# Every engine's queue in text order: a two-layer convolution kernel without its instruction planner

## The chip, the cores and the metric

The kernel runs on one core of a Trainium2 chip. The metric is the device time of one execution in microseconds, here 9654.11 us, the median of 3 runs (9645.51 to 9654.31). The engines are called as in the profile: PE (TensorE, matrix products), DVE (VectorE), ACT (ScalarE), POOL (GpSimd) and SP (SyncE, which only issues transfers). Each takes its instructions from a queue in a fixed order, and an instruction that waits holds up those behind it.

## The reference

Input x is 32 images of 96 channels, 56 x 56 points, fp32. Two layers follow each other.

```
# layer 0: expand, depthwise 3x3, squeeze-and-excite, project, residual (weights rounded to 8 bits)
h = silu(bn(conv1x1(x, q(w1))))                     # 96 -> 576 channels
h = silu(bn(depthwise3x3(h, q(w2))))
s = sigmoid(se_w2 @ silu(se_w1 @ mean(h) + b1) + b2)
x = x + bn(conv1x1(h * s, q(w3)))                   # 576 -> 96

# layer 1: attention from spectra, deformable 3x3 convolution, batch norm over all images
mag = abs(rfft2(x));  fe = mean over channels of mag, resized
ca  = sigmoid(mlp(pooled, separably filtered mag))               # one per channel
sa  = sigmoid(small convs of [mean(x), sqrt(mean(x*x)), fe])     # one per point
y   = x * ca * sa
freq_e = mean over channels of abs(rfft2(y)), resized
aux = [y, 4 coordinate planes, freq_e]
offset = conv3x3(aux);  gate = sigmoid(conv1x1(relu(conv3x3(aux))))
z = (1 - gate) * conv3x3(y) + gate * deformable_conv3x3(y, offset)   # bilinear samples
out = relu(batchnorm(z) + x)
```

## The kernel before

**Image pipeline.** Image b goes through three streams at once. *First* (`hidden`, L203) expands image b+2 with matmuls (`expand`, L168, silu on ACT L172) and runs the depthwise convolution on DVE: nine taps (L259, L261) for each of nine units of 128 channels, written to DRAM after a silu (`finish`, L221). *Second* (`attend`, L437) takes image b+1: squeeze (L284 to L296), projection in four steps of two row blocks (`project`, L323 and L329, with loads hq by SP and residuals on POOL), then the spectrum (`dft_mag`, L338: L386 and L410 on PE, squares on ACT L413, sums on DVE L372 and L414, roots L417), the chain of small steps that makes ca and sa (L477 to L557), a second spectrum with the gate (L366 on POOL), and freq_e (L564 to L578). The main loop (L1105) makes z of image b.

**Bands.** The main loop goes over bands of 8 rows, 7 an image. In each band `offsets` (L641) finds the offsets of the band two further on: convolution L605 (offsets, gate's hidden layer, a third of the base convolution), ACT L625 and L628, copies L651 on DVE, base convolution L633, and by way of DRAM the bilinear weights: `ht` (L667 on SP, L670 and L671 on ACT), `hd`, then `weights_load` (L685, L686 on SP) and their product L692 on DVE. A band has two halves. In each, `block_channels` (L696) cuts blocks of y on POOL (L703) and transposes them on PE (L707, out by ACT L709), `sample_tiles` samples by matmul (L721, out by ACT L725) in two groups of three and four tiles, `pack` (L732) moves a third of the taps, and `deform` (L740) makes the product, one half later. `combine` (L779 to L782) ends a band on DVE. The rows of y for the next image are loaded and weighted by `refill` (L584, L592, freq_e L596).

**Slots.** After each tile of a sampling group, and three times at the end of a band, `pump` (L1012) makes a slot: 17 in a band. In a slot each stream takes as many steps as its share of the image's slots asks for; a step ends at a `yield`. At the sixth band of an image (`turn`) the streams move on by one image.

**What sets the order.** The text gives SP's order alone (L1351). For PE, DVE, ACT and POOL a planner of the framework orders the instructions when the kernel is built, by its own costs and by when inputs come free; one place is held to the text by name (L670). After the build each engine's order is fixed. PSUM has 8 banks: 6 that go round (`mm`), one (`acc`) for the small products of `attend`, one (`pd`) for L740.

```
    with tc.manual_schedule(engines={mybir.EngineType.SP}):
        layers(tc, a, dp, x1d, zd, stats, far)
```

Before the first band, image 0 goes through both streams with image 1's first stream beside it, 0.45 steps to one (`beside`, SPREAD). After the last band `normalise` reads all z again and writes the output.

Of the kernel before, what the change touches and what calls it, by code (L numbers as in the profile page):

```python
# [73 lines left out]
UNITS = [(c, 0) for c in range(4)] + [(4, None)] + [(c, 1) for c in range(4)]  # L74

# [127 lines left out]
def hidden(tc, p, x, xn, h2d, pooled, defer):  # L203
# [12 lines left out]
    for _ in expand(nc, p, xts, UNITS[0]):  # L216
        yield
# [8 lines left out]
    for u, (ch, half) in enumerate(UNITS):  # L226
        h1 = p["h1"]
        more = expand(nc, p, xts, UNITS[u + 1]) if u + 1 < len(UNITS) else iter(())
        if xn is not None and u in (5, 8):

            p.setdefault("xts", []).append(rows_of(xn, int(u == 8)))
        acc = p["acch"].tile([128, HH, W], FP, name="acch")
# [5 lines left out]
        if diag is not None:  # L238
# [9 lines left out]
            next(more, None)  # L248
            yield
        for n, k in enumerate(taps):  # L250
# [11 lines left out]
            if n % 2:  # L262
                if n == 3 and before:
                    finish(u - 1, before)
                next(more, None)
                yield
# [12 lines left out]
def squeeze(nc, p, pooled):  # L279
# [3 lines left out]
    for u, (ch, _) in enumerate(UNITS):  # L283
        nc.tensor.matmul(p1[:RED, 0:1], w["sew1"][:, ch], pooled[:, u : u + 1],  # L284
                         start=(u == 0), stop=(u == len(UNITS) - 1))
    s1 = p["sp"].tile([RED, 1], FP, name="s1")
    nc.scalar.activation(s1, p1[:RED, 0:1], AF.Silu, bias=w["seb1"], scale=1.0 / HW)
    yield
    for ch in range(NCH):
        nc.tensor.matmul(p1[:, 8 + ch : 9 + ch], w["sew2"][:, ch], s1, start=True, stop=True)  # L290
    s2 = p["sp"].tile([128, NCH], FP, name="s2")
    nc.vector.tensor_tensor(s2, p1[:, 8 : 8 + NCH], w["seb2"], ALU.add)
    nc.scalar.activation(s2, s2, AF.Tanh, scale=0.5)
    nc.vector.tensor_scalar(s2, s2, 0.5, 0.5, ALU.mult, ALU.add)
# [20 lines left out]
def project(nc, p, rows):  # L315
# [11 lines left out]
    for half in range(2):  # L327
        ps = slice(64 * half, 64 * half + 64)
        nc.tensor.matmul(pts[half][:C, :EW], w3s[ps, NCH - 1], both[ps], start=False, stop=True)  # L329
    outs = []  # L330
# [7 lines left out]
def dft_mag(nc, p, src, gate=None):  # L338

# [3 lines left out]
    if gate is None:  # L351
        parts = p["sq"].tile([2 * WX, 2, NPB * V], FP, name="sq")[: 2 * H, :, : NG * W].rearrange("p k (g w) -> p k g w", g=NG)
# [11 lines left out]
    def weigh(g):  # L364
        if gate is not None and g < NG:
            nc.gpsimd.tensor_tensor(x2s[g][:, :, :W], x2s[g][:, :, :W], gate.unsqueeze(1).to_broadcast([2 * H, CG, W]), ALU.mult)  # L366
# [9 lines left out]
    for _ in range(2):  # L376
        yield
# [3 lines left out]
    if gate is not None:  # L381
        yield
# [13 lines left out]
    if gate is None:  # L396
        p["sums"] = p["sp"].tile([2 * H, 2, W], FP, name="sums")
        nc.vector.tensor_reduce(p["sums"], parts.rearrange("p k g w -> p k w g"), AX.X, ALU.add)
    mag = s1[:, :, :V]
    n = NQB * V  # L400
    pairs = mag.rearrange("p (r q) u -> p r q u", r=2)
    for q0 in range(0, NP // 2, NQB):
# [9 lines left out]
        for r, pt in enumerate(pts):  # L412
            nc.scalar.activation(sq[:, r].rearrange("p k n -> p (k n)"), pt[:, : 2 * n], AF.Square)  # L413
        nc.vector.tensor_tensor(pairs[:, :, q0 : q0 + NQB], sq[:, :, 0].rearrange("p r (q u) -> p r q u", q=NQB),  # L414
                                sq[:, :, 1].rearrange("p r (q u) -> p r q u", q=NQB), ALU.add)
        yield
    nc.scalar.activation(mag, mag, AF.Sqrt)  # L417
    p["magnitude"] = mag


def resized_spectrum(nc, p, mag, name, scale=None):


    m2 = p["sp"].tile([2 * WX, V], FP, name=f"m_{name}")
    if scale is not None:
        nc.vector.tensor_tensor(mag, mag, scale.unsqueeze(2).to_broadcast([2 * WX, NP, V]), ALU.mult)
    nc.vector.tensor_reduce(m2, mag.rearrange("p q u -> p u q"), AX.X, ALU.add)
    yield
    pf = p["acc"].tile([128, 512], FP, name="acc")
    nc.tensor.matmul(pf[:V, : 2 * W], m2, p["w"]["RT2"], start=True, stop=True)  # L430
    rs = p["sp"].tile([V, 2, W], FP, name=name)
    nc.scalar.copy(rs.rearrange("p m w -> p (m w)"), pf[:V, : 2 * W])
    p["resized"] = rs
    yield


def attend(tc, p, b, x, h2d, pooled, x1, given=False):  # L437
# [7 lines left out]
    if not given:  # L445
        NQ = HH // ER
        first = project_loads(nc, p, h2d, 0, 0)
        yield from squeeze(nc, p, pooled)
        rows = [first, project_loads(nc, p, h2d, 0, 1)]
        for _ in range(2):  # L450
            yield
        for q in range(NQ):
# [5 lines left out]
            if q + 1 < NQ:  # L458
                first = project_loads(nc, p, h2d, q + 1, 0)
            yield  # L460
# [7 lines left out]
            yield  # L468
    yield
# [4 lines left out]

    s3 = p["sp"].tile([H, 2, W], FP, name="s3")
    pm = p["acc"].tile([128, 512], FP, name="acc")
    nc.tensor.matmul(pm[:H, : 2 * W], w["fold"], p["sums"].rearrange("p k w -> p (k w)"), start=True, stop=True)  # L477
    nc.scalar.activation(s3[:, 1], pm[:H, W : 2 * W], AF.Sqrt, bias=w["eps6"][:H], scale=1.0 / C)
    nc.scalar.mul(s3[:, 0], pm[:H, :W], 1.0 / C)
    yield  # L480
    yield from resized_spectrum(nc, p, mag, "fe")
    fe = p["resized"]
# [4 lines left out]
    nc.vector.tensor_reduce(edge[:, :, 5:], mag, AX.X, ALU.add)  # L487
    for m in range(2):
# [3 lines left out]


# [5 lines left out]
    pc = p["acc"].tile([128, 512], FP, name="acc")  # L499
    for k in range(3):  # L500
        nc.tensor.matmul(pc[:NP, 8 + 2 * k : 10 + 2 * k], qs[:, 0, k], w["two"], start=True, stop=True)
    g = p["sp"].tile([NP, 3, 2], FP, name="g")
    nc.scalar.copy(g.rearrange("p k c -> p (k c)"), pc[:NP, 8:14])
    yield
    for n in range(6):
        k, c = divmod(n, 2)
        nc.tensor.matmul(pc[: 2 * MID, 0:1], w["cp1"][:, k, c], g[:, k, c : c + 1], start=(n == 0), stop=(n == 5))
    c1 = p["sp"].tile([2 * MID, 1], FP, name="c1")
    nc.scalar.activation(c1, pc[: 2 * MID, 0:1], AF.Relu, bias=w["cp1b"])
    yield  # L510

    nc.tensor.matmul(pc[:C, 1:2], w["cp2"], c1[:MID], start=True, stop=True)
    c2 = p["sp"].tile([2 * MID, 2 * WX], FP, name="c2")
    nc.vector.tensor_scalar(c2, w["twoT"], c1, None, ALU.mult)
    ca = p["ca"].tile([C, 1], FP, name="ca")
    sigmoid(nc, ca, pc[:C, 1:2], w["half"]("cp2_b", C))
    p["ca", b] = ca
    yield
    nc.tensor.matmul(pc[: 2 * WX, 64 : 64 + NP], c2, w["cp2X"], start=True, stop=True)
    cx = p["sp"].tile([2 * WX, NP], FP, name="cx")  # L520
    nc.vector.tensor_tensor(cx, pc[: 2 * WX, 64 : 64 + NP], w["cp2bX"], ALU.add)
    nc.scalar.activation(cx, cx, AF.Tanh, scale=0.5)
    nc.vector.tensor_scalar(cx, cx, 0.5, 0.5, ALU.mult, ALU.add)


    p1 = p["acc"].tile([128, 512], FP, name="acc")
    t1 = p["sp"].tile([W, 3, H], FP, name="t1")
    for m in range(3):
        t = p1[:W, m * H : (m + 1) * H]
# [5 lines left out]
        nc.scalar.activation(t1[:, m], t, AF.Identity, bias=w["sdh_b"](m, W))  # L535
    yield
    p2 = p["acc"].tile([128, 512], FP, name="acc")
    s4 = p["s4"][b % 2]
    for m in range(3):
        nc.tensor.matmul(p2[:H, m * W : (m + 1) * W], t1[:, m], w["twT"][:, m], start=True, stop=True)  # L540
        nc.scalar.activation(s4[:, m, 1 : 1 + W], p2[:H, m * W : (m + 1) * W], AF.Identity, bias=w["sdw_b"](m, H))
    yield
    p3 = p["acc"].tile([128, 512], FP, name="acc")
    r = p["sp"].tile([H, 3, W], FP, name="r")
    for m in range(3):
        for dx in range(3):
# [92 lines left out]


def offsets(nc, p, yp, j, top, hid, ybs, hds):  # L641

    w = p["w"]
# [854 lines left out]
```

## Time and profile before

| | |
|---|---|
| median of 3 runs | 9654.11 us |
| profiled execution, its own time | 9648.5 us |
| its span, first to last instruction | 9646.7 us |
| PE busy | 8472.7 us (88%) |
| PE weight loads | 5064.2 us (52%) |
| DVE busy | 7227.2 us (75%) |
| ACT busy | 5322.1 us (55%) |
| POOL busy | 2532.6 us (26%) |
| PE clock granted, mean | 0.923 |
| DMA | 154 GB/s mean |
| last statistics of image 0, of image 31 | 798.2 us, 9360.7 us |

The profile is of one execution. Busy shares count matmuls, vector and scalar instructions; idle time before an instruction is put down to what released it. A row of a timeline is a run of like instructions. The normalisation fills the time after 9360.7 us.

### The profile page before, as it was taken

The numbers are of one execution on the slowest core, as the hardware profiler recorded it, in microseconds if no ns is written. First come the engines' busy times: TensorE is split into PE (matmuls) and PEld (weight loads), VectorE is DVE, ScalarE is ACT, GpSimd is POOL, SyncE is SP. The second block draws the span as 40 slices with busy tenths as digits, with TensorE's granted clock in tenths as the row PEclk, the third lists the DMA queues.
The fourth block names the chain that finished last, engine by engine and source line by source line (L and its number), as shares of the span: only waits on it lengthen the run. The fifth ranks groups of instructions, "written<-read, shape, count | busy, mean of one in ns | idle before, by whom it ended". The sixth has DMA issues, their size and how long they took to land. (4 is left out here: it accounts for less than half of the span.)

```text
span 9646.7 us, 129705 instructions
## 1 busy us (share of the span) xinstructions
PE 8472.7 (88%) x48374; PEld 5064.2 (52%) x48374; DVE 7227.2 (75%) x6948; ACT 5322.1 (55%) x10262; POOL 2532.6 (26%) x2642
## 2 busy tenths in 40 slices
PE   6889989998999999999899989999999999999870
PEld 3455555555555555555555555555555555555540
DVE  7688777778777787877777887777878777777323
ACT  2355555565555556555555655555555555565453
POOL 1123223222222322222232322233222323322210
PEclk9899999999999999999999999999999999999985
DMA  2355555555555555555555555555555555554449
GB/s 94 95 143 148 151 152 160 150 149 143 147 155 154 160 154 145 145 149 155 154 160 155 145 142 153 151 158 154 153 139 145 150 157 157 153 152 135 130 154 417
DMA packets 1069473, 1485.98 MB, mean 154 GB/s; under 512 B 590438, under 2 KB 840086, under 8 KB 1056550
## 3 DMA queue, kind: packets, MB, share of 16 engines
q1 hardware_dynamic: 858747, 985.20, 37.9%
q10 hardware_dynamic: 153803, 329.80, 9.2%
q0 software_dynamic: 56288, 162.60, 6.7%
q8 instruction: 388, 6.36, 0.3%
q14 instruction: 247, 2.02, 0.1%
HBM read 1064.29 MB, written 412.65 MB: 153 GB/s over the span
## 5 line engine op out<-in xcount | busy, mean ns | idle before, releaser
L261 DVE SCALAR_TENSOR_TENSOR acch<-hp,w,acch 128x1512 f32<-128x1512 f32 (+1 forms) x2250 | 4320.5, 1920 | 32.8
L605 PE MATMUL mm<-yp,c_jointW 104*128 104x448 f32 x4032 | 1649.0, 561 | 9.0 <-ACT yt L709 5.5
L740 PE MATMUL pd<-v,c_def 128*96 128x224 f32 (+1 forms) x6272 | 1414.8, 376 | 127.6 <-ACT v L732 104.1
L703 POOL COPY ybl<-yp 96x448 f32<-96x448 f32 x896 | 1014.7, 1159 | 1903.7 <-PE mm L707 1903.3
L721 PE MATMUL mm<-wc,yt 64*96 64x144 f32 x12544 | 1168.1, 308 | 153.5 <-DVE yb L638 76.8
L740 PEld LDWEIGHTS pd<-v,c_def 128*96 128x96 f32 (+1 forms) x6272 | 1051.8, 173 | 437.4 <-ACT v L732 142.5
L168 PE MATMUL mm<-xt,w 96*128 96x392 f32 (+3 forms) x2688 | 1136.3, 561 | 133.8 <-ACT yt L709 96.0
L605 PEld LDWEIGHTS mm<-yp,c_jointW 104*128 104x128 f32 x4032 | 783.6, 196 | 806.0 <-issue 762.6
L721 PEld LDWEIGHTS mm<-wc,yt 64*96 64x96 f32 x12544 | 884.2, 167 | 489.8 <-issue 188.0
L221 ACT ACTIVATE acch<-acch,sh,inv 128x1568 f32<-128x1568 f32 x288 | 487.5, 1693 | 1159.0 <-DVE acch L261 1143.9
L692 DVE TENSOR_TENSOR wc<-wc,wr 128x1008 f32<-128x1008 f32 x448 | 564.6, 1260 | 704.2 <-DMA wr<-hd 690.5
L725 ACT COPY v<-mm 96x288 f32<-96x288 f32 (+1 forms) x2688 | 1003.6, 442 | 117.7 <-PE mm L721 78.9
L172 ACT ACTIVATE hp<-mm,sh,inv 128x392 f32<-128x392 f32 (+2 forms) x1216 | 811.8, 672 | 326.9 <-PE mm L168 282.1
L633 PE MATMUL mm<-yp,c_base0W 96*64 96x448 f32 x4032 | 913.5, 550 | 0.0
L323 PE MATMUL mm<-hq,w3s 128*96 128x392 f32 x2048 | 788.2, 531 | 127.4 <-DMA hq<-h2d 125.9
L655 POOL DMA_DIRECT2D od<-at x224 | 186.3, 832 | 2275.1 <-DVE at L651 1451.9
L732 ACT COPY v<-v 32x448 f32<-32x448 f32 x1344 | 755.3, 562 | 30.3
L168 PEld LDWEIGHTS mm<-xt,w 96*128 96x128 f32 (+1 forms) x2688 | 389.9, 189 | 495.1 <-issue 264.8
L709 ACT COPY yt<-mm 128x384 f32<-128x384 f32 (+1 forms) x896 | 350.9, 441 | 491.5 <-PE mm L707 489.4
L323 PEld LDWEIGHTS mm<-hq,w3s 128*96 128x96 f32 x2048 | 336.3, 173 | 477.7 <-issue 382.5
L466 POOL TENSOR_TENSOR o<-o,xc 96x392 f32<-96x392 f32 x256 | 396.5, 1549 | 643.9 <-ACT o L333 642.3
L633 PEld LDWEIGHTS mm<-yp,c_base0W 96*64 96x64 f32 x4032 | 294.6, 134 | 515.5 <-issue 490.2
(194 smaller groups left out, 9023.7 us busy)
## 6 DMA issues: line engine op xcount, KB each, us to landing
h2d<-acch ACTq DMA_DIRECT2D x288, 784.0 KB
wc<-hd SPq DMA_DIRECT2D x896, 252.0 KB
wr<-hd SPq DMA_DIRECT2D x896, 252.0 KB
hq<-h2d SPq DMA_DIRECT2D x128, 980.0 KB
hq<-h2d SPq DMA_DIRECT2D x128, 784.0 KB
x<-x1d SPq DMA_DIRECT2D x768, 98.0 KB
ht<-od SPq DMA_DIRECT2D x224, 252.0 KB
hd<-ht ACTq DMA_DIRECT2D x224, 252.0 KB
```

The costliest lines, as they stand in the source:

```text
L168: nc.tensor.matmul(pt[p0 : p0 + w1.shape[1], : rows * W], w1, xts[hf][:, r0 * W : (r0 + rows) * W], start=True, stop=True)
L172: nc.scalar.activation(h1[lo:hi, row0 : row0 + rows, 1 : 1 + W], pt[lo:hi, : rows * W].rearrange("p (h w) -> p h w", h=rows), AF.Silu, bia ...
L261: nc.vector.scalar_tensor_tensor(acc[:, lo:hi], win, wk, acc[:, lo:hi], ALU.mult, ALU.add)
L323: nc.tensor.matmul(pts[half][:C, :EW], w3s[:, ch], hq, start=(i == 0), stop=False)
L605: nc.tensor.matmul(view, weights[:, k], yp[:channels, r0 : r0 + RB, dx + PD - 1 : dx + PD - 1 + W], start=(k == 0), stop=(k == NTAP - 1))
L633: nc.tensor.matmul(pb[k % 2 * BC : (k % 2 + 1) * BC, :BW].rearrange("p (h w) -> p h w", h=RB), w["base"][:, k], yp[:C, r0 : r0 + RB, dx + ...
L692: nc.vector.tensor_tensor(wc, wc, wr, ALU.mult)
L703: nc.gpsimd.tensor_copy(yb[:, :, s], blocks)
L721: nc.tensor.matmul(pt[k][:C, (t - lo) * KP : (t - lo + 1) * KP], yt[ps, t], s[ps, t * KP : (t + 1) * KP], start=True, stop=True)
L725: nc.scalar.copy(v[:C, :, lo:hi, k].rearrange("c k t p -> c t k p"), pt[k][:C, : (hi - lo) * KP].rearrange("c (t k p) -> c t k p", t=hi - ...
L732: nc.scalar.copy(v[C:, 1 + 2 * i : 3 + 2 * i], v[i * QC : (i + 1) * QC, KA:])
L740: nc.tensor.matmul(out.rearrange("c q (t x) -> c t q x", x=TS), p["w"]["def"][ks, k], v[ks, k].rearrange("c t s (r x) -> c t (s r) x", r=T ...
```

## The change

All four compute engines get text order too, and the text is rewritten:

- `pump`: *second* takes exactly one step a slot, *first* one tap's share of 81 steps; a step in `hidden` is now one tap, and the next unit is expanded during the last six taps, the next image's first unit during the last unit.
- In `attend`, `dft_mag`, `squeeze` and `project` an evacuation or a use stands one step after the product that it needs; the products of a chain share one `acc` bank in disjoint columns; the two halves of the chain (ca and sa) are interleaved; the loads of the second spectrum start before the first chain ends.
- `at_conv`: the square roots (and their table loads) wait until the next L605 has been written, then go behind it.
- `block_copies`: POOL cuts a half's blocks one half earlier. `prepare` for the bilinear weights moves from the start of a half to after its first group, and asks for one half more.
- `offsets`: the convolutions' evacuations get their own steps, with fewer steps before `ht`.
- `refill` for the next image's first rows moves from the turn to the second half of the band before it; the weighting of each row block comes 3, 4, 5 ... slots later.

```diff
-    with tc.manual_schedule(engines={mybir.EngineType.SP}):
+    with tc.manual_schedule():
...
+def at_conv(p, do):
+    if "at_conv" not in p:
+        do()
+        return
+    p["at_conv"].append(do)
+    while do in p["at_conv"]:
+        yield WAIT
...
-            if n % 2:
-                if n == 3 and before:
-                    finish(u - 1, before)
+            if n == 3 and before:
+                finish(u - 1, before)
+            if len(taps) - 8 < n < len(taps) - 1:
                 next(more, None)
-                yield
+            yield
...
-    nc.scalar.activation(mag, mag, AF.Sqrt)
     p["magnitude"] = mag
+    yield from at_conv(p, lambda: nc.scalar.activation(mag, mag, AF.Sqrt))
...
+    yield
+    for m in range(3):
+        nc.scalar.activation(t1[:, m], p1[:, m * H : (m + 1) * H], AF.Identity, bias=w["sdh_b"](m, W))
+    for k in range(3):
+        nc.tensor.matmul(pg[:, 2 * k : 2 * k + 2], qs[:, 0, k], w["two"], start=True, stop=True)
+    yield
+    g = p["sp"].tile([NP, 3, 2], FP, name="g")
+    nc.scalar.copy(g.rearrange("p k c -> p (k c)"), pg)
+    for m in range(3):
+        nc.tensor.matmul(p2[:, m * W : (m + 1) * W], t1[:, m], w["twT"][:, m], start=True, stop=True)
+    yield
+    s4 = p["s4"][b % 2]
+    for m in range(3):
+        nc.scalar.activation(s4[:, m, 1 : 1 + W], p2[:, m * W : (m + 1) * W], AF.Identity, bias=w["sdw_b"](m, H))
+    for n in range(6):
+        k, c = divmod(n, 2)
+        nc.tensor.matmul(pcs[0][: 2 * MID], w["cp1"][:, k, c], g[:, k, c : c + 1], start=(n == 0), stop=(n == 5))
+    yield
...
-    p["tc"].keep_in_program_order(nc.scalar.activation(ht, ht, AF.Abs, bias=w["blk"]))
+    yield from wait(4)
+    nc.scalar.activation(ht, ht, AF.Abs, bias=w["blk"])
     nc.scalar.activation(ht, ht, AF.Relu, bias=w["one"], scale=-1.0)
...
-                due = st[2] * min(1.0, (slot - st[3]) / (st[4] - st[3]))
+                due = slot - st[2] if len(st) == 3 else n_first * (slot - st[2]) / st[3]
                 while st[1] < due:
+                    if next(st[0], None) is WAIT:
+                        break
                     st[1] += 1
-                    next(st[0], None)
+                    if len(st) == 3:
+                        break
...
-                later.append((slot + 4, lambda args=args: attend_rows(nc, p, b, *args)))
+                later.append((slot + 3 + n, lambda args=args: attend_rows(nc, p, b, *args)))
...
             next(more, None)
+            release()
             for h in range(2):
                 v = p["vp"].tile([128, NTAP, NTH, 2, TP], FP, name="v")
-                prepare(2 * n + h + READY + AHEAD)
...
-                        if h == 1 and n + 1 < len(bands):
-                            yts.append(block_channels(nc, p, yp, bands[n + 1][1], 0))
+                        if blocks:
+                            yts.append(block_channels(nc, p, blocks.pop()))
+                        if 2 * n + h + 2 < len(halves):
+                            blocks.append(copies(2 * n + h + 2))
                         ready.extend(weights(nc, *ws) for ws in loads[:1])
                         del loads[:1]
-                        if h == 0:
-                            yts.append(block_channels(nc, p, yp, j, 1))
+                        prepare(2 * n + h + READY + AHEAD + 1)
+                        if b + 1 < B and j == turn - 1 and h == 1:
+                            refill(b + 1, turn * RB - PD)
```

## The prediction

> **What bounds the kernel now.** I read the busy rows first, then the waits of TensorE (PE), then the timeline of one image.
>
> A stretch of 29 images, 1083.60 to 9222.30 us (columns: length; PE, weight loads, DVE, ACT, POOL busy; PE clock; DMA share; GB/s):
>
> ```profile
> 1083.60:9222.30 8138.70, 7466.42 (x43220) 4471.16 (x43219) 6293.93 (x5860) 4673.15 (x9109) 2270.97 (x2353) 0.94 0.54 150
> ```
>
> An image takes 8138.70 / 29 = 280.6 us. PE is idle for (8138.70 - 7466.42) / 29 = 23.2 us of it, and a clock of 0.94 loses another 0.06 x 280.6 = 16.8 us. With no gap and a full clock PE would need 240.6 us. DVE is busy for 217.0 us, ACT for 161.1 us. So PE is the bound, and what it can gain is 40 us an image. DVE, at 217 of 240.6, isn't far behind.
>
> What ended PE's gaps, and two large waits of other engines (us in total, times, longest):
>
> ```profile
> PE mm L323 <- DMA hq<-h2d: 125.9, 31, 9.4
> ...
> PE mm L168 <- ACT yt L709: 96.0, 44, 5.2
> PE mm L707 <- ACT sq L413: 80.3, 21, 6.5
> ...
> PE acc L430 <- DVE m_fe L427: 43.1, 31, 4.2
> PE acc L430 <- DVE m_fy L427: 40.0, 30, 2.9
> ...
> ACT acch L221 <- DVE acch L261: 1143.9, 185, 12.7
> DVE wc L692 <- DMA wr<-hd: 690.5, 152, 18.3
> ```
>
> One place of one image, in order of time (start, length, instruction, idle time before it):
>
> ```profile
> 3116.44 1.21 DVE L692 TENSOR_TENSOR wc<-wc,wr 128x1008 f32<-128x1008 f32 x1 [8.04 <-DMA wr<-hd]
> 3117.56 0.63 DVE L414 TENSOR_TENSOR s<-sq 128x464 f32<-128x464 f32 x1
> 3118.29 1.01 ACT L413 ACTIVATE sq<-mm 128x464 f32<-128x464 f32 x2 [7.90 <-DVE s L414]
> ...
> 3118.90 0.47 PE L707 MATMUL mm<-c_ident,ybl 96*128 96x96 f32 x3 [4.28 <-ACT sq L413]
> ...
> 3120.76 1.28 ACT L417 ACT_TABLE_LOAD   x1
> ...
> 3123.88 1.68 PE L168 MATMUL mm<-xt,w 96*128 96x392 f32 x2 [1.26 <-ACT yt L709]
> ...
> 3126.72 0.55 PE L430 MATMUL acc<-c_RT,m_fe 128*29 128x112 f32 x2 [1.17 <-DVE m_fe L427]
> ...
> 3128.67 9.32 PE L605 MATMUL mm<-yp,c_jointW 104*128 104x448 f32 x18
> ```
>
> The root of the 4.28 us gap is a transfer: DVE stood 8.04 us before the weights' product L692, the magnitudes' sum L414 was queued behind it, the square L413 waited for that sum, and PE for the bank. The square root with its table load then holds ACT. The convolution L605 takes 9.32 us here and 7.02 elsewhere, so the gaps are paid twice, as the clock shows:
>
> ```profile
> 3124.00:3128.67 4.67, 3.50 (x7) 1.40 (x8) 4.67 (x5) 4.61 (x11) 0.00 (x0) 0.50 0.00 0
> 3128.67:3137.91 9.24, 9.24 (x19) 4.19 (x17) 7.46 (x7) 2.78 (x6) 0.00 (x0) 0.75 0.34 85
> 3137.91:3163.68 25.77, 25.31 (x183) 16.15 (x183) 24.93 (x31) 17.97 (x43) 7.18 (x6) 1.00 0.62 152
> ```
>
> Over the stretch, 16.8 us of clock go with 23.2 us of idle: 0.72 us for each.
>
> The last row matters as much: from 3137.91 to 3163.68 nearly the whole attention chain (L501 to L549) ran, and PE was busy 25.31 of 25.77 us. The planner had filled each step's latency with sampling, packing and base-convolution work.
>
> **What the change removes.** The roots go behind L605 (7.02 us on PE, which covers 1.28 + 1.41 us of ACT). The weights' loads are issued two thirds of a half-band earlier on SP, behind the sampling that frees their buffers. This takes most of L707 (80.3), L168 (96.0) and L430 (83.1): 259.4 / 32 = 8.1 us of idle an image. The hq loads (125.9 / 32 = 3.9) lose about 3, as at two of three places more PE work now lies between release and use. Together 11 us, with their clock 11 x 1.72 = 19 us an image.
>
> **What it adds.** Each engine's queue is now the text. A chain step goes one to a slot, but slots aren't equal: three or four stand after each sampling group, and seven at the end of a band, with only expansion matmuls (L168, 0.76 us a piece) between them. I lay PE, ACT and DVE side by side through the seven bands of one image, with the trace's durations: L605 7.0 us, L633 4.0, L740 2.65, L707 0.67, L721 1.15 or 0.91, L763 0.83; ACT L725 1.29 or 0.93 a group, L709 0.78, L732 1.7 for three, L172 0.67, L221 1.88, L754 1.15, L636 0.63; DVE L261 1.84, L692 1.2, combine (L779 to L782) and L662 3.3.
>
> 1. *Mean-spectrum chain, 11.7 us.* After the last L721 of its half ACT still owes 0.7 us of L725, L636 0.63 and the copy of fe 0.3, and L531 follows L721 at once: 1.7 us of PE idle. Then the table goes back (1.28), L172 (0.67) and three L535 (0.9) stand ahead of what L501 waits for, against 0.76 of PE work: 1.7. Before L507 ACT has L221 1.88, L172 0.67, L732 1.7, L754 1.15, L725 0.93 and three L541 0.9 = 7.2; PE has L540 0.7, L168 0.76, L763 0.83, L721 0.91 = 3.2: 4.1 with the handovers. L547, L512, L519 each wait for an evacuation of the same bank: 1.1, 1.1, 1.2; two of 0.4.
> 2. *Start of the next image's offsets, about 10 us.* Its first L605 needs y's first rows, weighted on DVE by L592. Between L638 and that L592 DVE's text has the combine and L662 3.3, six L261 11.0, one L692 1.2 and L592 itself twice 1.3 = 16.8 us; PE has 8.4 us of sampling, deformed convolution and expansion. With small ACT waits in it the gap is near 9.8. In the trace of before the planner put L592 in the middle of the taps. The waiting L605 holds up everything on PE; ACT's evacuations for it follow.
> 3. *Squeeze, 5.2 us.* L290 behind L287, which has L732, L754 and L725 ahead of it: 1.9; the scaled weights L296 behind DVE's taps: 2.5; the next hq load, issued after the last matmul that reads the buffer, with 3.6 us of PE work against some 4.2 from release to landing: 0.8.
> 4. *First transform, 6.5 us.* The third tile's reload: 2.6; L410 waits for a square's sum L372, behind the combine and 1.6 us of other sums on DVE: 3.9.
> 5. *The other bands, 4 us*: L572 1.3, L740 behind a late L732 1.3, hq 1.0, and 0.4.
>
> Sum: 38 us of idle, against 23.2. The edits that only split a step (the halves of the sigmoid, one bank for a chain's products) add no instruction, and their waits are in these numbers. L221's wait (1143.9 us) goes too: in the text it stands a unit's fourth tap behind its end. That is no gain of its own, only less in ACT's queue. POOL's block copies (1.16 us each, two a half-band) move to a half-band ahead of their transposes, some 20 us (280.6 / 14), which hides them; without that cover a pair is 2.3 us of PE.
>
> **Clock.** [...] The row shows half clock after gaps of 1.26 and 1.17 us; at 0.72 the loss would be 27 us. But where DVE or ACT sets the end of a wait, a slower PE only fills it. I take half, 13.5.
>
> **Sum.** 240.6 + 38 + 13.5 = 292.1 us an image, 11.5 more than now: 29 x 11.5 = 334 us. The first image's chain runs before the bands, at 0.45 steps of the next image's convolution to one of its own, and had 529 us with PE busy 385; in text order some of the planner's filling goes: +40, between -20 and +80. The last two images and the normalisation: 0. From the profiled execution's span of 9646.7: 9646.7 + 374 = 10,021. That execution took 9648.5 and the median is 9654.1, so I add 7: about 10,030.
>
> **Rivals.**
> - *Faster.* ACT and DVE queues may run further ahead than I laid them, so that waits of 1 to 2 us vanish. With 19 us won and new idle of 12 us without clock loss an image takes 273.6: 29 x -7, 9,450. For it: the 8.04 us DVE waits go, and DVE then has slack. Against: L507's 7.2 us of ACT work behind a data-bound L540, and 16.8 us of DVE work before L592, don't depend on slack. It decides where PE's idle of an image stays under the 23.2 us of now.
> - *Balanced.* New idle of 23 to 26 us: 9,600 to 9,750. L592's wait may shrink when DVE has caught up.
> - *Transfers become the bound.* Projection's 16 steps took 16 x 108/61 = 28 slots, now 16, so 1.7 MB of hq, residuals and stores fall in 4 slots. SP's queue is in order; if each of 8 hq loads is 1.5 us late, with the weights behind them and their clock, it is 20 us an image more: 10,600. Against it: DMA share 0.54, and the projection's bands hold 43 us of PE work.
>
> **How the numbers follow.** Slower by 9,800 to 10,350: 0.56; transfers or clock worse, above 10,350: 0.10; balanced 0.12 (0.06 slower, 0.03 same, 0.03 faster); faster 0.22, half of it below 9,500. A difference under 0.2% (19 us) can't be told from none. So faster 0.25, same 0.03, slower 0.72. The range 9,500 to 10,380 leaves about 0.2 out. The likeliest case has 9,800 to 10,350.
>
> **What would show it.** Right: no PE wait for squares or roots near the mean chain; new PE gaps at L507, L531 and L501's places ended by ACT, of 1 to 4 us; the first offset convolution of each image waiting for L592 by 5 to 11 us; PE clock at or below 0.94; idle of PE over 30 us an image. Wrong: if DVE runs ahead at L592, or the slots' chain steps find ACT empty, PE's idle falls under 20 us and the kernel is faster.

## The result and the profile after

| | before | changed |
|---|---|---|
| median | 9654.21 us | 10185.85 us |
| profiled execution's span | 9646.7 us | 10205.2 us |
| ratio to before | | 1.0552, 95% interval 1.0531 to 1.0574 |
| steady image (29 of them) | 280.6 us | 297.9 us |
| of it PE idle, PE busy | 23.2, 257.5 us | 39.9, 258.1 us |
| statistics of image 0 | 798.2 us | 828.1 us |

The changed kernel is 5.5% slower: 532 us, where 376 us were forecast (10,030 us). The time is inside the stated range of 9,500 to 10,380 us. Line numbers of the changed kernel differ from those of before: L605 is L632 now, L592 is L619, L386 is L407, L410 is L432, L323 is L351, L531 to L519 are L518 to L563, L707 is L724, L168 is L186, L430 is L501 and L593, L721 is L738, L740 is L757, L261 is L286.

The windows view for 29 steady images, columns as before (length; PE, weight loads, DVE, ACT, POOL busy; clock; DMA share; GB/s):

```profile
1129.00:9769.20 8640.20, 7483.69 (x43199) 4567.74 (x43199) 6278.71 (x5854) 4664.93 (x9102) 2245.66 (x2354) 0.90 0.53 141
```

PE's busy time is the same within 0.6 us an image, and so are DVE's (216.5) and ACT's (160.9). Nearly all that the loop lost is idle time of PE: 39.9 - 23.2 = 16.7 of 17.3 us an image. Over 29 images the loop accounts for 501.5 us of the spans' difference of 558.5; the head up to image 1's statistics for 45.4, the end for 11.6.

What ended PE's gaps (total, times, longest):

```profile
PE mm L632 <- DMA yp<-fqd: 296.2, 27, 12.6
PE mm L407 <- DMA x<-x1d: 224.9, 56, 6.9
PE mm L351 <- DMA hq<-h2d: 105.9, 76, 4.9
PE acc L538 <- ACT s L535: 69.1, 32, 2.5
PE mm L632 <- ACT hp L190: 64.6, 29, 2.2
...
PE mm L632 <- DVE acch L286: 59.9, 5, 12.7
...
PE acc L316 <- ACT s L313: 55.6, 32, 3.2
PE acc L518 <- ACT fe L508: 46.9, 31, 1.5
```

None of the gaps that bounded the kernel before is left but hq: the waits of L724, L186 and of the reductions for L501 and L593 are gone in the loop. In their place stand two large ones (the turn at L632, the first transform at L407) and the row of small ones of the mean chain. DVE stood 690.5 us for the weights before; all its idle time ahead of the product L704 is some 25 us now.

The turn in one image, in order of time (start, length, instruction, idle before it):

```profile
4302.10 5.97 DVE L286 SCALAR_TENSOR_TENSOR acch<-hp,w,acch 128x1568 f32<-128x1568 f32 x3
4304.88 0.93 PE L186 MATMUL mm<-xt,w 96*128 96x392 f32 x2
4308.00 1.19 DVE L704 TENSOR_TENSOR wc<-wc,wr 128x1008 f32<-128x1008 f32 x1
4309.11 3.67 DVE L286 SCALAR_TENSOR_TENSOR acch<-hp,w,acch 128x1568 f32<-128x1568 f32 x2
4313.50 0.62 SPq L623 DMA_DIRECT2D yp<-fqd  x1
4313.70 0.68 DVE L619 SCALAR_TENSOR_TENSOR yp<-yp,ca,sab 96x448 f32<-96x448 f32 x1 [0.92 <-DMA yp<-x1d]
4314.54 0.68 DVE L619 SCALAR_TENSOR_TENSOR yp<-yp,ca,sab 96x448 f32<-96x448 f32 x1 [0.16 <-DMA yp<-x1d]
...
4317.24 1.08 PE L632 MATMUL mm<-yp,c_jointW 104*128 104x448 f32 x1 [11.43 <-DMA yp<-fqd]
```

PE has nothing from 4305.8 on. DVE works through taps and one weights' product up to 4312.8 before its first weighting; that is the forecast's step. But the frequency row is issued only at 4313.50 and lands after the weightings. A view that names one releaser names the transfer, and hides that DVE's text alone would have kept PE waiting until some 3 us before it did start. Which is it? The experiments ask that first.

### The profile page after: what moved, and what is told of

Same layout as the page of the kernel before. It is cut to its first block, busy times and chain, and to the rows that moved or that the text cites. A ratio compares the mean times of both kernels' runs of the same rounds, so it can differ in the third digit from the quotient of the medians.

```text
span 10205.2 us, 129758 instructions
## 1 busy us (share of the span) xinstructions
PE 8493.2 (83%) x48374; PEld 5169.5 (51%) x48374; DVE 7226.4 (71%) x6948; ACT 5318.3 (52%) x10264; POOL 2490.8 (24%) x2642
## 5 line engine op out<-in xcount | busy, mean ns | idle before, releaser
L286 DVE SCALAR_TENSOR_TENSOR acch<-hp,w,acch 128x1512 f32<-128x1512 f32 (+1 forms) x2250 | 4222.5, 1877 | 37.8
L632 PE MATMUL mm<-yp,c_jointW 104*128 104x448 f32 x4032 | 1729.9, 585 | 420.7 <-DMA yp<-fqd 296.2
L757 PE MATMUL pd<-v,c_def 128*96 128x224 f32 (+1 forms) x6272 | 1431.1, 385 | 64.4 <-DVE z L796 61.4
L632 PEld LDWEIGHTS mm<-yp,c_jointW 104*128 104x128 f32 x4032 | 812.3, 204 | 1261.0 <-issue 1158.4
L757 PEld LDWEIGHTS pd<-v,c_def 128*96 128x96 f32 (+1 forms) x6272 | 1098.7, 179 | 427.3 <-issue 130.6
L190 ACT ACTIVATE hp<-mm,sh,inv 128x392 f32<-128x392 f32 (+2 forms) x1216 | 801.2, 673 | 892.1 <-PE mm L186 702.3
L186 PE MATMUL mm<-xt,w 96*128 96x392 f32 (+3 forms) x2688 | 1058.2, 546 | 51.6 <-DMA xt<-in_x 45.6
L738 PE MATMUL mm<-wc,yt 64*96 64x144 f32 x12544 | 1053.4, 302 | 31.5 <-ACT hp L190 16.3
L738 PEld LDWEIGHTS mm<-wc,yt 64*96 64x96 f32 x12544 | 837.8, 166 | 351.2 <-issue 175.8
L670 PE MATMUL mm<-yp,c_base0W 96*64 96x448 f32 x4032 | 974.5, 585 | 0.0
L351 PE MATMUL mm<-hq,w3s 128*96 128x392 f32 x2048 | 740.5, 508 | 137.1 <-DMA hq<-h2d 105.9
L661 DVE COPY at<-mm 18x224 f32<-18x224 f32 x448 | 154.4, 380 | 972.8 <-ACT yb L657 970.2
L407 PE MATMUL mm<-c_FU,x 112*128 112x116 f32 x3072 | 443.6, 299 | 264.9 <-DMA x<-x1d 224.9
L241 ACT ACTIVATE acch<-acch,sh,inv 128x1568 f32<-128x1568 f32 x288 | 487.5, 1693 | 300.4 <-DVE acch L286 287.2
L704 DVE TENSOR_TENSOR wc<-wc,wr 128x1008 f32<-128x1008 f32 x448 | 591.8, 1321 | 25.0 <-PE mm L724 9.4
```

The lines of the kernel that those rows point to most:

```text
L186: nc.tensor.matmul(pt[p0 : p0 + w1.shape[1], : rows * W], w1, xts[hf][:, r0 * W : (r0 + rows) * W], start=True, stop=True)
L190: nc.scalar.activation(h1[lo:hi, row0 : row0 + rows, 1 : 1 + W], pt[lo:hi, : rows * W].rearrange("p (h w) -> p h w", h=rows), AF.Silu, bia ...
L286: nc.vector.scalar_tensor_tensor(acc[:, lo:hi], win, wk, acc[:, lo:hi], ALU.mult, ALU.add)
L351: nc.tensor.matmul(pts[half][:C, :EW], w3s[:, ch], hq, start=(i == 0), stop=False)
L632: nc.tensor.matmul(view, weights[:, k], yp[:channels, r0 : r0 + RB, dx + PD - 1 : dx + PD - 1 + W], start=(k == 0), stop=(k == NTAP - 1))
L670: nc.tensor.matmul(pb[k % 2 * BC : (k % 2 + 1) * BC, :BW].rearrange("p (h w) -> p h w", h=RB), w["base"][:, k], yp[:C, r0 : r0 + RB, dx + ...
```

## The experiments

Medians; each ratio is to the kernel before, run beside it (medians 9,659 to 9,668 us). "Image" is the steady image, of which so much PE idle.

| | median us | ratio, 95% interval | image, idle us |
|---|---|---|---|
| changed kernel | 10185.85 | 1.0552 (1.0531-1.0574) | 297.9, 39.9 |
| row loads early | 10089.0 | 1.0447 (1.0426-1.0468) | 294.1, 35.9 |
| whole refill early | 10070.82 | 1.0434 (1.0414-1.0453) | 293.3, 33.9 |
| two blocks early | 10193.24 | 1.0538 (1.0506-1.0570) | 298.2, 35.1 |
| taps paced by band | 10048.84 | 1.0407 (1.0378-1.0436) | 293.5, 34.1 |
| transform spread | 9898.66 | 1.0247 (1.0221-1.0272) | 287.1, 30.5 |
| chain spread | 10540.83 | 1.0907 (1.0881-1.0933) | 308.9, 46.6 |
| four edits together | 10123.21 | 1.0486 (1.0457-1.0515) | 295.4, 35.3 |
| roots inline | 11067.07 | 1.1450 (1.1423-1.1478) | 327.1, 60.5 |
| new text, planner | 10441.65 | 1.0809 (1.0784-1.0835) | 306.5, 38.6 |
| old text, text order | 10547.73 | 1.0920 (1.0901-1.0939) | 308.8, 42.2 |
| new text, DVE planned | 10768.77 | 1.1149 (1.1117-1.1181) | 316.3, 49.6 |
| before, weights' loads moved | 9858.77 | 1.0192 (1.0164-1.0220) | 287.2, 25.5 |

### The turn: DVE's text or the transfers

**Row loads early.** SP issues the rows half a band earlier; masks and weightings stay.

```diff
+    if (b, r0) not in p.setdefault("loaded", set()):
         nc.sync.dma_start(rows, ...)                     # load_rows
...
+    if 0 < b + 1 < B and j == turn - 1 and h == 0 and ("fq", b + 1) in p:
+        for r in range(0, turn * RB - PD, RB): nc.sync.dma_start(yp[rows r...], x1d[b + 1]...)
+        load_freq(nc, p, yp, b + 1, 0, turn * RB - PD)
```

> The changed kernel, but SP issues the next image's first five row blocks and the frequency row half a band earlier; their masks and the weightings on DVE (L619) stay at their place in the text. Theory A, as the prediction has it (DVE's text ahead of L619 sets the end): the 11.5 us stall at the turn falls only to about 8.4 us, the 3 us by which the frequency row came after the weightings; 10,186 - 29 x 3 = about 10,100. Theory B (late transfers set it): the stall falls under 4 us and the time to about 9,950.

The stall at the turn, in this kernel's own lines (L633 is the convolution, L620 the weighting, L705 the weights' product):

```profile
4238.93 7.84 DVE L286 SCALAR_TENSOR_TENSOR acch<-hp,w,acch 128x1568 f32<-128x1568 f32 x4
...
4243.58 0.93 PE L186 MATMUL mm<-xt,w 96*128 96x392 f32 x2
4246.70 1.20 DVE L705 TENSOR_TENSOR wc<-wc,wr 128x1008 f32<-128x1008 f32 x1
4247.81 3.67 DVE L286 SCALAR_TENSOR_TENSOR acch<-hp,w,acch 128x1568 f32<-128x1568 f32 x2
4251.40 1.27 DVE L620 SCALAR_TENSOR_TENSOR yp<-yp,ca,sab 96x448 f32<-96x448 f32 x2
4252.18 4.05 PE L633 MATMUL mm<-yp,c_jointW 104*128 104x448 f32 x5 [7.67 <-issue]
```

("issue" means that the profile names no releaser.) No transfer is waited for now: DVE runs six taps and the product without a pause, and PE starts where the first of its two weightings ends. Over the run the stall is 245.1 us in 30, 8.2 each; in the changed kernel it was 296.2 us in 27 and 59.9 in 5, 11.1 each. The median fell by 97 us; Theory A expected 8.4 us and 10,100. So 8 us of the stall are DVE's text, as the forecast had it, and 3 us the transfers.

**Whole refill early, and two blocks of it.** Here the weightings move with the loads.

```diff
-    if b + 1 < B and j == turn - 1 and h == 1:
+    if b + 1 < B and j == turn - 1 and h == 0:           # whole refill early
         refill(b + 1, turn * RB - PD)
...
+    if b + 1 < B and j == turn - 1:                       # two blocks early
+        refill(b + 1, turn * RB - PD if h else 2 * RB)
```

> As the changed kernel, but the whole refill of the next image's first rows (loads, masks, and with them the weightings on DVE) starts half a band earlier. Both theories: the stall of 11.5 us goes, 29 x 11.5 = 334 us at most, with its clock perhaps more: 9,800-9,900. If a new wait takes its place (DVE standing at a weighting whose row block has not landed, with the taps behind it), less than half of that: above 10,020.

> The changed kernel, but only the two row blocks that the next image's first offset convolution reads (and their 16 values of the frequency row) are loaded and weighted half a band earlier; the other three stay. Theory A (the stall is DVE text ahead of the weightings plus 3 us of transfer): the 11.5 us stall goes and, with two mask buffers for two blocks, DVE no longer stands at a mask with the weights' product behind it, as it does in the run with all five blocks early: 10,186 - 334 = about 9,850. Rival (each earlier weighting only moves the wait to DVE): 10,050 or more.

In both the 11 us stall is gone; the time fell by 115 us with the whole refill early and not at all with two blocks early. With the whole refill early the weights' product stands behind a weighting on DVE and the sampling waits: L738 went from under 1 to 6.7 us an image. With two blocks early, the band after the turn shows this:

```profile
4931.89 0.51 POOL L613 DMA_DIRECT2D sab<-sad  x1 [6.46 <-DVE yp L619]
...
4938.46 0.56 DVE L619 SCALAR_TENSOR_TENSOR yp<-yp,ca,sab 96x336 f32<-96x336 f32 x1 [4.57 <-issue]
4938.94 1.78 DVE L286 SCALAR_TENSOR_TENSOR acch<-hp,w,acch 128x1512 f32<-128x1512 f32 x1
4940.76 1.69 ACT L241 ACTIVATE acch<-acch,sh,inv 128x1568 f32<-128x1568 f32 x1 [15.17 <-DVE acch L286]
...
4942.94 0.93 ACT L742 COPY v<-mm 96x432 f32<-96x432 f32 x2 [0.40 <-ACT acch L241]
4943.51 0.74 PE L724 MATMUL mm<-c_ident,ybl 96*128 96x96 f32 x3 [6.86 <-ACT v L742]
```

DVE is late with the taps, ACT stands 15.17 us at a unit's end, and the evacuation queued behind it keeps PE's banks. Part of DVE's lateness is a wait of its own: the 4.57 us stand before the fifth weighting L619, for its mask `sab`. There are two mask buffers; POOL issues this load at 4931.89, when an earlier weighting has freed one, and it lands at 4938.38. The two bands around the turn, from the windows view, first of the changed kernel, then with two blocks early:

```profile
4278.52:4317.24 38.72, 26.54 (x147) 15.68 (x146) 34.12 (x27) 23.48 (x44) 7.99 (x10) 0.87 0.72 172
4317.24:4363.39 46.15, 41.61 (x200) 24.63 (x201) 33.88 (x30) 18.51 (x37) 9.82 (x15) 0.89 0.72 180
```

```profile
4893.71:4920.83 27.12, 26.37 (x147) 15.85 (x146) 22.95 (x22) 19.31 (x38) 6.05 (x6) 1.00 0.71 170
4920.83:4975.94 55.11, 44.79 (x202) 26.57 (x200) 44.16 (x36) 23.25 (x45) 16.11 (x17) 0.81 0.74 183
```

84.9 and 82.2 us for the pair in these two images, 85.6 and 86.0 us in the mean over 24. DVE has 68.0 and 67.1 us of work in these two. Take the stall at L632 away, and PE meets a late DVE 20 us later through ACT. Whether DVE is late by its load or by its own waits for masks and rows isn't settled: ahead of L619 it stands 294.5 us over the run of the changed kernel and 205.6 us with two blocks early, and a third mask buffer was not tried.

**Taps paced by band.** If that is so, moving DVE's work should help where moving waits did not.

```diff
-    due = slot - st[2] if len(st) == 3 else n_first * (slot - st[2]) / st[3]
+    due = slot - st[2] if len(st) == 3 else taps(NBD * (slot - st[2]) / st[3])
+    TAPS = (12, 16.5, 12, 9.5, 13, 10.5, 7.5)             # taps() runs through this sum, one value a band
```

> The changed kernel, but the 81 taps of an image are spread over its seven bands as 12, 16.5, 12, 9.5, 13, 10.5, 7.5 instead of 11.6 each: fewer where PE has little work beside them (DVE 34.7 us beside some 25 us of PE in the last band), more where PE has 44 us. Theory C (DVE's load against PE's by band sets the time there, so that clearing one wait only moves it): the sum over bands of the longer of the two falls by some 8 us, 29 x 8 = 232 us: about 9,950. Theory A (single waits, each worth what its gap shows): the turn's stall loses the taps ahead of the weightings, 2 of 1.9 us: 10,080 at best. If neither, 10,150-10,250.

137 us less: more than half of Theory C's 232, and somewhat above the 106 that Theory A allowed at best. L632 has one wait of 8.9 us in place of two with 13.7; the taps ahead of the turn's weightings are among those moved. L407 has 4.2 us in place of 8.1, which the edit doesn't touch directly. That fits Theory C in part, but doesn't isolate DVE: a step of `hidden` also expands the next unit on PE (L186) and ACT (L190), so their work moved between the bands too, and 34.1 us of idle stay.

### The mean chain and the first transform

**Chain spread.** One more step between an evacuation and its product at eight places.

```diff
     for m in range(3):
         nc.scalar.activation(t1[:, m], p1[...], AF.Identity, ...)
+    yield
     for k in range(3):
         nc.tensor.matmul(pg[:, 2 * k : 2 * k + 2], qs[:, 0, k], w["two"], ...)
```

> The changed kernel, with one more step between an evacuation and its product at eight places of the mean chain (L518, L526, L531, L538, L544, L550, L569 and the product before the second tanh). Theory A (each gap is ACT's queue being longer than PE's work of one slot): of 8.4 us idle in the chain some 2 remain, 29 x 6.4 = 186 us: about 10,000. Rival (the gaps come from slots that hold nearly no PE work, so that they stay wherever the steps fall): 10,130 or more. The second roots come a band later; nobody waits for them by either theory.

A miss by 540 us for Theory A, in the wrong direction; the rival's "10,130 or more" holds. The gaps didn't close: they are 9.2 us in sum against 8.4, one of them 4.73 (the product L534 behind the evacuation L531). In one image PE has 0.93 us of expansion in the slots before L534, and then stands 4.87 us. And everything behind the chain moved by 8 slots: the second transform's steps now wait for POOL's scaling (248.3 us in all, 5.5 in the changed kernel), so that L407 has 15.0 us an image. One step can't be shifted alone in this text.

**Transform spread.**

```diff
-        yield from wait(2)
+        yield from wait(4)                                # before the first tile of the first transform
...
         nc.scalar.copy(s1..., pt...)
         yield
+        if gate is None:
+            yield
```

> The changed kernel, with the first transform two slots later and its six steps two slots apart, so that the reload of a tile has twice the PE work beside it. Theory A: the waits of L407 for its tiles fall from 8.1 us to about 2 us an image, 29 x 6 = 177 us: about 10,010. Rival (the reload is late because SP and the transfer engines are full of weights' loads there, whatever the step): L407 keeps 5 us or more, time above 10,090.

L407's waits fell from 8.1 to 1.8 us, as Theory A said, and the median by 287 us where 177 were expected. More came from L632, which has one wait of 8.2 us now instead of two with 13.7 us, though the edit doesn't touch it; why was not traced. The best of the variants of the changed kernel, still 2.5% behind the kernel before.

**Four edits together**: the spread transform, the early row loads (without the frequency row), one more step in each quarter of the projection ahead of the residual, and one more ahead of the squeeze's second product.

```diff
+            yield
             for k, o, xr in zip(at, os, xrs):
                 nc.gpsimd.tensor_tensor(o, o, xr, ALU.add)
```

> The changed kernel with the transform's steps spread (as in the run that gave 9,899), the five row blocks issued on SP half a band earlier, one more step a projection quarter between the hq loads and their use, and one more step before the squeeze's second product. If the gaps are local (Theory A): against 9,899 the turn loses 3 us, hq 3 us, the squeeze 1.4 us an image, 29 x 7.4 = 215 us: about 9,690, level with the kernel before. If the turn is bound by DVE's load in those two bands (68 us of DVE work in 86 us), whatever waits first: the gain is under half of it, 9,800 or more.

225 us slower than the spread transform alone, where the rival said 9,800 or more. The waits aimed at shrank (turn 6.7, hq's line 3.3, of it 0.5 named as the transfer, squeeze 1.5 us), but the transform's steps moved with the projection's, and their waits for a tile are back:

```profile
PE mm L408 <- DMA x<-x1d: 192.3, 26, 9.3
PE mm L637 <- DVE yp L624: 154.4, 23, 11.0
PE mm L408 <- DVE sq L392: 67.2, 28, 2.7
PE mm L408 <- DVE acch L286: 54.3, 7, 8.4
```

The first wait of 7.4 us an image (192.3 in 26) is for a tile that SP could issue only when DVE had summed the one before it (SP waited 461.4 us there, 61.2 in the changed kernel; but also 308.9 with the transform spread alone, where this gap is missing, so SP's wait is not the whole cause). At the turn DVE is named now, not the transfer.

### What the change took away

**Roots inline.** The square roots where the transform ends.

```diff
         do()
         return
+    do()
+    return
     p["at_conv"].append(do)
```

> The changed kernel with the square roots (and their table loads) at once where the transform ends, not behind the next offset convolution. Theory A, as in the prediction (a root with its two table loads, 1.28 + 1.41 + 1.28 us on ACT, holds up evacuations): +3 to +8 us an image, 10,270-10,420. Rival (in text order ACT reaches the root only when PE is already waiting for something else, or the convolution that should hide it isn't near): within 10,186 +- 30.

```profile
5165.20 1.28 ACT L443 ACT_TABLE_LOAD   x1
5166.49 1.40 ACT L443 ACTIVATE s<-s 128x1392 f32<-128x1392 f32 x1
5167.91 1.28 ACT L192 ACT_TABLE_LOAD   x1
5167.93 2.54 DVE L492 TENSOR_REDUCE m_fe<-s 128x29 f32<-128x1392 f32 x1 [2.60 <-ACT s L443]
...
5170.02 1.28 ACT L495 ACT_TABLE_LOAD   x1
...
5171.77 0.58 PE L503 MATMUL acc<-c_RT,m_fe 128*29 128x112 f32 x2 [11.77 <-ACT s L496]
```

880 us slower, against an upper end of 234: of the parts tried alone in text order this is worth by far the most. The two gaps behind the roots are 11.7 and 7.8 us an image (L503, L595); in the changed kernel they are gone. Between the magnitudes' root and the next one ACT goes back to the other table: 5.9 table loads of 1.28 us an image in place of 4.0.

**The weights' loads, in the kernel before.**

```diff
-    prepare(2 * n + h + READY + AHEAD)
...
+    prepare(2 * n + h + READY + AHEAD + 1)               # after the half's first group
```

> The kernel before, planner and all, with one part of the change alone: the weights' loads are issued after the first sampling group of a half instead of at its start, and one half further ahead. By the prediction's step of what is removed (the weights' late arrival at the root of the gaps at L707, L168 and part of L430, some 5 of the 8.1 us an image, with their clock 1.72 times that): 29 x 8.6 = 250 us less, about 9,400. Rival (in the planned order these waits are only where DVE's slack shows; what PE waits for next stands right behind them): 9,600-9,700. If the later loads upset the planner's order: above 9,700.

The sign is wrong: 1.9% slower, the third of the outcomes written down. Two of the waits it aims at do shrink (L707 from 2.7 to 1.3 us an image, hq at L323 from 4.0 to 0.2), but L168 and L430 stay, and DVE waits for the weights as long as before (734.3 us against 690.5). SP's queue tells why:

```profile
SPq L685 <- DMA hd<-ht: 1569.4, 130, 26.9
```

It was 702.6 us. Asked for half a band further ahead, the source isn't written yet, and SP stands before it; what is behind in its queue, the tiles of x among it, comes later: the transform L386 waits 5.9 us an image for tiles that POOL scales (0.8 before). The sampling L721 waits 8.2 us (4.5 before). In the changed kernel SP stands just as long (1,639.1 us).

### Text and order, apart

**New text with the planner; old text in text order.** The edit is the one line `manual_schedule`, in the one and the other.

> The changed text, but the planner again orders PE, DVE, ACT and POOL; SP's order is the text's, as in both kernels. Theory A (the in-order compute engines cost the time: 8.4 us of mean-chain gaps, and vector work standing ahead of the row weightings): the planner fills those gaps again, PE idle falls from 39.9 us to 20-26 us an image and the time to 9,500-9,750. Theory B (the transfers come late because of where the rewritten text issues them on SP: the 11 us turn stall, the 8 us at the first transform, 4 us of hq): the planner can't move an SP instruction, only the chain's 8 us go, PE idle stays at 30 us or more and the time at 9,900-10,000.

> The text of before with all five engines in text order (its one line held to program order becomes an ordinary line). Both theories: the old text puts each evacuation straight behind its product, so every such pair stalls: I expect 60-120 us more idle an image than before and 11,500-13,500 us. If it comes out near 10,190, the rewriting of the text was worth nothing.

| us | planner | text order |
|---|---|---|
| old text | 9,654 | 10,548 |
| new text | 10,442 | 10,186 |

Both expectations missed. In text order the new text is worth 362 us, so the rewriting does what it is meant to; but it costs the planner 787. The planner did close the mean chain (L501 to L563 have 0.6 us an image in place of 8.4) and the turn (1.0). What came in their place:

```profile
PE mm L724 <- ACT v L742: 243.9, 28, 10.9
PE mm L186 <- ACT yt L726: 138.2, 48, 5.6
...
ACT s L320 <- DVE s L319: 653.7, 31, 25.3
```

ACT stands 21 us at each squeeze's tanh for one short sum on DVE (187.5 us in 32 in the changed kernel), with PE's evacuations behind it. Theory A, that the planner would win back the time by filling the new text's gaps, is wrong; that this one wait explains the 787 us wasn't tried.

**New text, DVE alone planned.**

```diff
-    with tc.manual_schedule():
+    with tc.manual_schedule(engines={mybir.EngineType.SP, ...PE, ...Activation, ...Pool}):
```

> The changed text in text order on PE, ACT, POOL and SP, while the planner orders DVE alone. Theory A: the weightings and sums that PE waits for go ahead of taps, the turn's 8 us and some of the chain's gaps go: 9,850-9,980. Rival, after the run with all four engines planned (10,442): the planner puts small DVE steps behind taps where the in-order ACT waits for them: 10,250 or more.

583 us slower than text order. The turn and the chain kept their gaps; L738, with under 1 us in the changed kernel, got 12.6:

```profile
PE mm L738 <- DVE at L661: 228.6, 36, 10.9
PE mm L738 <- ACT sq L435: 112.6, 30, 5.7
```

The copy of the offsets L661, which frees the convolution's bank, stands behind taps in that order: in one image ACT's last step for it ends at 4246.65, DVE then does seven taps and a product, copies at 4260.28, and PE starts after 8.03 us of idle. Why the planner ranks it so was not tried.

## Why the prediction was right

Slower, and in the main by the mechanism stated: PE's idle time grows where a product follows DVE's or ACT's text. At the first transform and for a part of the turn it is transfers instead. Step by step, in us of idle an image:

| step of the prediction | forecast | measured |
|---|---|---|
| old gaps removed (L707, L168, L430) | 8.1 | 8.3, all of them |
| hq, 3.9 before | 1.8 in the sum of what is added | 4.1, of it 3.2 for the transfer |
| 1 mean chain | 11.7 | 8.4 |
| 2 next image's first offsets | 9.8-10 | 11.6 |
| 3 squeeze, without hq | 4.4 | 1.7 |
| 4 first transform | 6.5 | 8.1 |
| 5 others, without hq | 3 | 6.0 |
| all, with hq | 38 | 39.9 |
| PE busy above 240.6, put down to the clock | 13.5 | 17.5 |
| image | 292.1 | 297.9 |

The total is closer than its parts: the chain and the squeeze came out 3.3 and 2.7 us too high, the turn, the transform, hq and the others 1.7, 1.6, 2.3 and 3.0 too low. That these nearly cancel is luck. The forecast's own five items also add up to 37.2 us, not 38. And its account of what goes leaves out another 6 us: the waits of L740 and L721, 8.5 us an image before, are 2.5 at L757 and L738.

- **Chain**: the places and their order are right one by one (L518 1.51 against 1.7, L526 1.37 against 1.7, L544 0.89 against 1.1, L550 0.78 and L563 1.09 against 1.1 and 1.2). Only the largest was overestimated, L538 with 2.2 for 4.1.
- **Turn**: mechanism shown by the early row loads (8.2 us are DVE's). Mis-sized by the transfers, 3 us, which the sum left out: SP's five row loads stood behind the weights' loads, behind POOL's block copies (last section) and behind one another. What the forecast didn't say is that the stall isn't worth its length; two runs took it away and got 115 us and nothing.
- **First transform**: the place is right, the parts are not. L410's wait for a sum, 3.9 us, didn't come. Instead both waits are for tiles: 2.7 us in the mean for the first tile, whose load follows the store of the projection's rows, and 5.7 for a reloaded one, for which 2.6 were forecast. In one image that reload is issued at 4435.16 and used at 4441.07, 5.9 us. So this sum was nearly right for a wrong reason.
- **Squeeze and projection**: the scaled weights' 2.5 us didn't come; hq was to lose 3 of 3.9; its wait for the transfer fell only to 3.2, and 0.9 for ACT's evacuations came at the same line. The added PE work between release and use shortened the wait by 0.8 us.
- **Not foreseen**: L632 of the band behind, 2.2 us, for a bank that ACT L190 has not left.
- **Head**: +29.9 us at image 0's statistics, +45.4 at image 1's, for +40.

**Clock.** The forecast's rate, 0.72 us of clock for one of idle, does not hold up. It rests on a floor of 240.6 us of PE work, found by taking (1 - 0.94) of the whole image as lost. The same sum on the changed kernel gives 297.9 x 0.90 - 39.9 = 228.2 us, for the same matmuls. The mean clock also counts stretches in which PE is idle (from 4311.5 to 4317.2, in the changed kernel's turn, PE does nothing and the clock is 0.50), so neither floor is a measurement, no run shows the forecast's 13.5 us as a loss by the clock, and "17.5" above only says that PE's busy time is 258.1. Measured is this: idle grew by 16.7 us an image and the clock fell from 0.94 to 0.90, and PE's busy time grew by 0.6. The reason given in the forecast, that a slow PE ahead of a wait for DVE or ACT only fills the wait, isn't isolated by any run. That the halved estimate came within 4 us is luck.

The forecast also read one row wrongly. It set half clock "after gaps of 1.26 and 1.17 us". In the kernel before, the clock was at half already when those gaps came; it fell earlier, behind the gap of 4.28 us, in which it was 1.00, and was 0.50 from 3119.70 on:

```profile
3114.62:3118.90 4.28, 0.01 (x1) 0.00 (x0) 1.76 (x2) 0.61 (x2) 0.00 (x0) 1.00 0.21 69
3119.70:3124.00 4.30, 3.04 (x19) 2.01 (x17) 4.22 (x3) 4.25 (x6) 2.76 (x2) 0.50 0.00 0
```

In the changed kernel a shorter gap does stand before half clock. The rows hold a gap of 2.23 us, a stretch with none, one with a gap of 1.51 us, and what follows it:

```profile
1449.15:1451.38 2.23, 0.00 (x1) 0.00 (x1) 0.00 (x0) 1.79 (x4) 0.00 (x0) 1.00 0.65 254
1451.40:1467.00 15.60, 15.60 (x72) 9.21 (x73) 14.60 (x14) 9.05 (x16) 0.81 (x1) 1.00 0.35 82
1467.00:1470.90 3.90, 2.38 (x29) 1.91 (x28) 3.81 (x7) 3.69 (x9) 2.09 (x2) 1.00 0.56 127
1470.90:1491.00 20.10, 14.89 (x71) 8.67 (x71) 15.20 (x17) 10.39 (x25) 0.00 (x0) 0.50 0.58 142
```

The longer gap left the clock at 1.00 and the shorter one did not, so here the length of a single gap doesn't decide.

Against the sum's own span of 10,021 us the measured 10,205.2 is 184 more: 168 from 29 images of 5.8 us (1.9 of idle, 4 of PE's busy time), 5 from the head, 12 from the end. The terms that failed as a whole are small: L410's 3.9 us and the scaled weights' 2.5. The rival "faster" fell by the sign it named, idle under 23.2 us; measured are 39.9. "Transfers become the bound" described a real part (the turn's 3 us, the tiles, hq), without becoming the bound in the bands it named.

No run is faster than the kernel before. What stays open is why the planner does badly with the new text: one wait was seen, not tried by itself.

## What to carry to other kernels

When an engine follows the text, look at its work and its own waits over stretches of a few tens of us before pricing single waits of the bound engine: a wait at which a late engine is met can be taken away without gain, because it is met again later (with two blocks early the 11 us stall went, and 10,186 us became 10,193). In a written order the position of each step in its band is part of the tuning, so an edit that inserts steps has to be priced for all that stands behind it. A load asked for earlier than its source is written holds up those behind it in SP's queue: with the weights' loads moved, SP stood 1,569.4 us before their source in place of 702.6, and the transform waited 5.9 us an image in place of 0.8.

## What was not expected of the hardware

An entry in SP's queue that looks like a long issue can be a wait. In the changed kernel's turn five loads of rows stand there (minimum, median, maximum in ns):

```profile
L611 SPq DMA_DIRECT2D yp<-x1d x5: 448/626/8301, 4300.3 to 4312.8; - x5
```

One of them held the queue for 8.30 us from 4301.41 on, another for 2.9. The frequency row stands behind them. The first 5.0 of the 8.30 us are put down to POOL, which was still copying blocks out of the rows to be overwritten, until 4306.4. The change had moved both these copies and the loads. Over the run such waits take 4.1 us each (114.3 in 28):

```profile
4302.46 3.97 POOL L714 COPY ybl<-yp 96x448 f32<-96x448 f32 x2 [7.45 <-PE mm L724]
SPq L611 <- POOL ybl L714: 114.3, 28, 6.3
```

For the other 3.3 us and the 2.9 the profile names no releaser. In the 8.30 us the transfer engines' share was 1.00, where the loop's average is 0.53:

```profile
4301.41:4309.71 8.30, 3.65 (x27) 2.20 (x25) 8.19 (x6) 5.65 (x12) 4.95 (x4) 0.86 1.00 202
```

What held the issue for this rest no run shows.
